# Four edits to a one-core kernel of eight layers: operand fills, a store queue, a causal mask and the spreading of routing weights

## The chip, the cores and the metric

The kernel runs on one core of a Trainium2 chip, in one launch. The metric is device time in microseconds, the median of several runs. Before the change three runs took 2757.15, 2762.11 and 2770.57 us; the median is 2762.11.

The engines are named as in the profile: PE is TensorE (matrix products and transposes), DVE is VectorE, ACT is ScalarE, POOL is GpSimd and SP is SyncE, which here only issues DMA transfers. In the code they are called PE, V, S, G and nc.sync; nc.scalar.dma_start puts a transfer on ScalarE's own queue (ACTq).

## What is computed

The input x has 32 sequences of 64 tokens with 256 channels, so 2048 rows of 256 float32 numbers; ctx has the same shape. Eight residual layers follow each other:

```python
x = x + L0_xattn(layernorm(x), ctx, ctx, gamma)
x = x + L0_ffn(layernorm(x), ...)          # silu(gate) * up, then down
x = x + L1_xattn(layernorm(x), ctx, ...)   # 16 heads, quantised q, k, v and weights
x = x + L1_ffn(layernorm(x), ...)          # causal attention with rotary embedding, then 4 experts
x = x + L2_xattn(layernorm(x), ctx, ...)   # banded attention
x = x + L2_ffn(layernorm(x), ...)          # quantised gated unit
x = x + L3_xattn(layernorm(x), ctx, ctx)   # sigmoid attention
x = x + L3_ffn(layernorm(x), ...)          # 8 routed experts and a shared one
```

Three of them are touched by the change:

```python
# L0_xattn: 8 heads of 8 over the 64 rows of a sequence; attention runs over the 256 columns
qk = einsum('bhdq,bhdl->bhql', qh, kh) / sqrt(8)
ret = gamma * einsum('bhql,bhdl->bhdq', softmax(qk), vh)

# L1_ffn, attention: 16 heads of 128 over the 64 tokens of a sequence
scores = where(causal, einsum('bhqd,bhkd->bhqk', rope(q), rope(k)) / sqrt(128), lowest)
out = einsum('bhqk,bhkd->bhqd', softmax(scores), v) @ wo + bo

# L3_ffn: top 2 of 8 experts of width 176, and a shared expert of width 352
scores = softmax(x @ gate_w.T); topk_w, topk_i = top_k(scores, 2)
eo = einsum('eni,eih->enh', silu(x @ w_gate[e]) * (x @ w_up[e]), w_down)
y = einsum('ne,enh->nh', combine, eo) + (silu(x @ sw_gate) * (x @ sw_up)) @ sw_down
```

Here combine holds, for each token, its two weights at the places of its two experts and zero elsewhere.

## The kernel before, in words

The 2048 rows lie in SBUF as 16 tiles (NT) of 128 tokens, in 4 groups (NG) of 512. The layers are stages named A to H: A is L0_xattn, B L0_ffn, C L1_xattn, D L1_ffn (attention, then experts), E L2_xattn, F L2_ffn with G (L3_xattn) interleaved, H L3_ffn. The weights of a stage are requested while the stage ahead of it runs.

**Stages A and E** share attention_slots (L339), which is a manual schedule: the order of each engine's instructions is the order in which the Python code emits them, 8 slots per tile. For tile i, prepare starts 2 slots ahead, the scores for the row maxima (score_maxima, L235, products L251, reductions negm L255) start at slot 16, the attention itself (attend_unit, L274, products L283) at slot 30 and the product with the values (product_unit, L301) at slot 32. Up to three tiles are thus in flight. Products in full float32 are avoided by splitting queries and keys into three bfloat16 pieces on GpSimd (stacked, L195). The pieces are written to DRAM (d3k and d3q, one transfer per piece, five for the keys and three for the queries, L212) and read back as rows of the operand tiles stk and stq (stack_rows, L215, three transfers of 24 rows each for the keys and three for the queries). All of these go through nc.sync, one after the other. The negated maximum of each row is added by the same product: it is transposed, copied by ScalarE (nmr, nm; L263, L264), split on GpSimd and sent by ScalarE's queue into rows 96 to 98 of stq (L271). The operand tiles have 128 rows. There are four pairs, used in turn (i % 4), and operand_buffers (L152) fills their rows 64 to 127 once, stk with 1.0 and stq with 0.0. In A, VectorE does so by V.memset (L158), within prepare of tiles 0 to 3 (L432). In E the fill is a transfer from a row tile that first_of_E makes (L1293 to L1296). DMA transfers signal their end through semaphores that they share in turn, so a transfer also waits for the previous one on its own semaphore. ScalarE's other work at A's start is small: the copies of the transposed context into vmo (L457), the maxima (L263, L264, L271), and then the exponentials L287.

**D's attention** (run_D_attention, L1028) is not in a manual schedule: the framework's scheduler orders each engine's instructions from the dependencies. It has 64 units, 16 heads by 4 groups. The loop emits for unit u: product of u-4, transposed of u-3, scores of u-2, output, projections of u, inputs of a later group, values. In scores (L1094) a mask product of the identity with a bfloat16 mask tile, causalb (L1039), opens the accumulation of sp, and the four 128x128 score products add to it (L1100). VectorE takes the maximum (L1102), subtracts it (L1104), ScalarE takes the exponential of all 512 columns in one instruction (L1105), and VectorE sums (L1107), takes the reciprocal (L1108) and multiplies (L1109). transposed (L1112) then needs s on TensorE. In projections (L1073), VectorE forms rtq and rtk (L1084), and ScalarE writes the half-swapped copies rwq and rwk (L1087, two instructions each). ScalarE also copies v (L1071), pT (L1118) and oT (L1133), and in the first units hnT (L949).

**F and H.** F's parts are issued from a table (L1669 to L1688). Towards its end it also steps the first routing of H (routed_H for group 0), and the generator owners (L1757, by way of heads["owner"] at L1683), which makes the tile owner in three ScalarE copies. owner holds, in 32-row blocks, a 1 where a column of the 1408 routed columns belongs to expert e. routed_H (L1765) normalises a group, makes xnT and the routing weights, transposes those to 8 rows of 512 tokens, and splits them in three bfloat16 pieces in the tile share (rows 0, 32 and 64 onwards). run_H (L1809) goes through 4 groups of 14 chunks of 128 columns: chunks 0 to 10 are routed experts (176 columns per expert, so that some chunks span two experts), 11 to 13 the shared one. Each chunk has the products pgate and pup (L1844), for a routed chunk the product cb of owner and share (L1848), which spreads each token's weight of the column's expert over the partitions, and the down products hout of the chunk ahead of it (L1820). ScalarE makes sl = silu(pgate) (L1852), VectorE hm = pup * sl (L1854) and for a routed chunk hm * cb (L1856). After chunk 13 VectorE adds hout to x (L1827), and at the very end of the program 16 transfers write the output (L1892).

Of the kernel before, what the change touches and what calls it, by code (L numbers as in the profile page):

```python
# [17 lines left out]
P = 128  # L18
T = 2048
D = 256  # L20
# [11 lines left out]
def tile_net(ctx: ExitStack, tc: tile.TileContext, a: dict, out: bass.AP):  # L32
# [119 lines left out]
    def operand_buffers(pool, k, b, row=None):  # L152

        pair = {}
        for kind, value in (("k", 1.0), ("q", 0.0)):
            pair[kind] = pool.tile([P, 16, D], BF, name=f"st{kind}{b}")
            if row is None:
                V.memset(pair[kind][64:P], value)  # L158
            else:

                nc.sync.dma_start(pair[kind][64:P], bc(row[kind][64:P], 1, [64, 16, D]))
            yield
# [31 lines left out]

    def stacked(pool, k, dram, src, kind, i):  # L195
# [15 lines left out]
        for t in range(n):  # L211
            nc.sync.dma_start(d3[t].rearrange("d h c -> h d c"), t3[:, t % 3, :])  # L212
        return d3

    def stack_rows(k, d3, kind, i):  # L215
        st = k["st"][i % 4][kind]
        for m in range(3):
            first = 0 if kind == "q" else m
            src = d3[first : first + 3].rearrange("t d h c -> (t d) (h c)")
            nc.sync.dma_start(st[24 * m : 24 * m + 24], src)  # L220
# [807 lines left out]
    def run_D_attention(w, side, hs):  # L1028
# [4 lines left out]
        with ExitStack() as es:  # L1033
# [5 lines left out]
            causal = tpool.tile([P, 4, P], BF, name="causalb")  # L1039
            V.tensor_copy(causal, bc(w["causal"], 1, [P, 4, P]))  # L1040
# [53 lines left out]
            def scores(u):  # L1094
                qr, kr = qks.pop(u)
                sp = psum.tile([P, 4, P], F32, tag="sp", name="sp")
                PE.matmul(sp, identb, causal, start=True, stop=False, skip_group_check=True)
                for j in range(4):
                    js = slice(j * P, (j + 1) * P)
                    PE.matmul(sp[:, j, :], qr[:, js], kr[:, js], start=False, stop=True, skip_group_check=True)  # L1100
                mx = pool.tile([P, 4], F32, name="mx")
                V.tensor_reduce(mx, sp, AX.X, ALU.max)  # L1102
                s = pool.tile([P, 4, P], F32, name="s", bufs=3)
                V.tensor_tensor(s, sp, bc(mx, 2, [P, 4, P]), ALU.subtract)  # L1104
                S.activation(s, s, AF.Exp, scale=scale)  # L1105
                sm = pool.tile([P, 4], F32, name="sm")
                V.tensor_reduce(sm, s, AX.X, ALU.add)  # L1107
# [178 lines left out]
    def first_of_E(w, psum):  # L1286
# [5 lines left out]
        for kind, value in (("k", 1.0), ("q", 0.0)):  # L1292
            row[kind] = cp.tile([P, D], BF, name=f"row{kind}")  # L1293
# [139 lines left out]
    def run_F(w, side):  # L1433
# [12 lines left out]
        with tc.tile_pool(name="Ft", bufs=1, side=side) as tpool, tc.tile_pool(  # L1446
# [231 lines left out]
            for t in range(NT + 8):  # L1678
                for part, lag in parts:
                    if 0 <= t - lag < NT and (with_g or not part.__name__.startswith("g_")):  # L1680
                        part(t - lag)
                    if with_g and t >= NT + 1 and part.__name__ == "gained":
                        next(heads.get("owner", head), None)  # L1683
# [44 lines left out]
    def load_H(wp):  # L1728
# [18 lines left out]
        owner = w["owner"] = wp.tile([96, 1408], BF, name="owner")  # L1747
        heads["owner"] = owners(owner)

        w["xnT"], w["share"] = [], []  # L1750
        for b in range(2):
            w["xnT"].append(wp.tile([P, 2, 512], F32, name=f"xnT{b}"))
            w["share"].append(wp.tile([96, 512], BF, name=f"share{b}"))
# [3 lines left out]
    def owners(owner):  # L1757
        for t in range(3):
            rows = slice(32 * t, 32 * t + 32)
            S.copy(  # L1760
                owner[rows].rearrange("p (e i) -> p e i", i=176), bc(ident[rows, 32 * t : 32 * t + 8], 2, [32, 8, 176])
            )
            yield

    def routed_H(w, g, pool, psum, tags, big):  # L1765

        xnT, sh = w["xnT"][g % 2], w["share"][g % 2]
        if g < 2:
            G.memset(sh, 0.0)
# [29 lines left out]
        src = tp[0:8].rearrange("e j t -> e (j t)")  # L1799
        r = pool.tile([8, 512], F32, name="shr")  # L1800
        t = pool.tile([8, 512], BF, name="sht")
        S.copy(sh[0:8], src)
        V.tensor_tensor(r, src, sh[0:8], ALU.subtract)
        G.tensor_copy(t, r)
        G.tensor_copy(sh[32:40], t)
        G.tensor_tensor(sh[64:72], r, t, ALU.subtract)
        yield

    def run_H(w, side):  # L1809


        with ExitStack() as es:
            pool = es.enter_context(tc.tile_pool(name="Hw", bufs=2, side=side))
            psum = es.enter_context(tc.tile_pool(name="Hp", bufs=1, space=PSUM))
            owner = w["owner"]
            for _ in heads.pop("owner"):
                pass
            def down(g, ch, m, hm, outs):
                for j in range(4):
                    PE.matmul(  # L1820
                        outs[j // 2][:, j % 2, :], hm[:m, j * P : (j + 1) * P], w["down"][:m, ch, :],
                        start=ch == 0 and j % 2 == 0, stop=ch == 13, skip_group_check=True,
                    )
                if ch == 13:
# [9 lines left out]
            for g in range(NG):  # L1834
# [133 lines left out]
```

## Time and profile before

| measure | value |
|---|---|
| median of three runs | 2762.11 us (2757.15 to 2770.57) |
| the profiled execution | 2769.85 us, of which its span is 2768.1 us |
| ACT busy in the span | 1532.9 us |
| mean granted TensorE clock | 0.977 of full |
| DMA | 227.89 MB moved, mean 82 GB/s |
| first 25 us | PE busy 0.36, DVE 13.18, ACT 0.00, POOL 14.31 us |
| 25 to 60 us | PE busy 18.65, DVE 30.95, ACT 3.29, POOL 10.73 us |
| 60 to 280 us (rest of A) | PE busy 208.61 us of 220 |
| 1204 to 1820 us (D's attention) | PE busy 602.68, DVE 338.68, ACT 331.80, POOL 340.35 us of 616 |
| 2270 to 2430 us (late F) | PE busy 117.46 us of 160, granted clock 0.89 |

The profile is of one execution, and its times count from the start of the span. The page gives for each engine its busy time, and then the span in 40 equal slices of 69 us, each digit being the busy share of one slice in tenths (9 is 90% or more). A timeline row gives start, duration, engine, line, operation, the tile written and the tiles read, the shape and how many instructions were folded into the row; in brackets stands how long the engine had been idle before, and what released it. Durations of matrix products overlap, since TensorE has the next under way before the last has left: two starts in a row tell what a product costs, its duration does not. In the rows for windows the columns are the length and the busy time of PE, PEld (weight loads), DVE, ACT and POOL with the numbers of instructions, then the granted clock, the share of the DMA engines' time and GB/s.

### The profile page before, as it was taken

The numbers are of one execution on the slowest core, as the hardware profiler recorded it, in microseconds if no ns is written. First come the engines' busy times: TensorE is split into PE (matmuls) and PEld (weight loads), VectorE is DVE, ScalarE is ACT, GpSimd is POOL, SyncE is SP. The second block draws the span as 40 slices with busy tenths as digits, with TensorE's granted clock in tenths as the row PEclk, the third lists the DMA queues.
The fourth block names the chain that finished last, engine by engine and source line by source line (L and its number), as shares of the span: only waits on it lengthen the run. The fifth ranks groups of instructions, "written<-read, shape, count | busy, mean of one in ns | idle before, by whom it ended". The sixth has DMA issues, their size and how long they took to land.

```text
span 2768.1 us, 44270 instructions
## 1 busy us (share of the span) xinstructions
PE 2414.7 (87%) x15971; PEld 1431.1 (52%) x16078; DVE 1856.7 (67%) x3913; ACT 1532.9 (55%) x2181; POOL 1534.5 (55%) x1764
## 2 busy tenths in 40 slices
PE   4999889777777777779999999999888877789999
PEld 2555344344444444436666666666555544455565
DVE  7878555799999999955454554655577758833232
ACT  1666321699999999836555555534254557731111
POOL 4565533588888888865555555513488866710000
PEclk9999999999999999989999999999999998989999
DMA  6543000599999999930000000051343311000000
GB/s 166 133 116 86 24 1 1 120 204 204 202 204 200 203 206 201 204 106 1 16 8 23 8 1 1 1 107 52 79 99 90 93 46 55 1 0 8 8 8 8
DMA packets 618919, 227.89 MB, mean 82 GB/s; under 512 B 547494, under 2 KB 608844, under 8 KB 614092
## 3 DMA queue, kind: packets, MB, share of 16 engines
q1 hardware_dynamic: 615628, 224.26, 37.1%
q8 instruction: 127, 2.08, 0.3%
q10 hardware_dynamic: 3072, 0.79, 0.2%
q14 instruction: 92, 0.75, 0.1%
HBM read 66.91 MB, written 18.87 MB: 31 GB/s over the span
## 4 chain that ended last, share of the span: by engine, by line
PE 47%; DVE 19%; issue 9%; POOL 6%; ACT 2%; DMA 1%; ACTq 0%; POOLq 0%; DVEq 0%
DVE e L844 11%; PE yp L1141 4%; PE ppq L1082 4%; PE ppk L1082 4%; PE pgate L1844 4%; PE pup L1844 4%; PE hout L1820 3%; PE vp L1070 3%; POOL e L295 2%; PE sp L1100 2%; PE op L1126 2%; PE hmp L1198 2%; PE ep L1211 2%; PE sc L816 1%; PE op L805 1%
## 5 line engine op out<-in xcount | busy, mean ns | idle before, releaser
L868 ACT ACTIVATE ei<-e,nb,sq 128x2048 int16<-128x2048 f32 x256 | 535.4, 2092 | 39.6 <-DVE nb L865 35.0
L878 POOL CAST eb<-ei 128x2048 bf16<-128x2048 int16 x256 | 482.0, 1893 | 110.7 <-ACT ei L868 92.7
L816 PE MATMUL sc<-kT,qz 128*128 128x512 bf16 x930 | 281.0, 381 | 154.6 <-DVE e L844 150.6
L255 DVE TENSOR_REDUCE negm<-s 128x2 f32<-128x512 f32 (+1 forms) x512 | 300.7, 610 | 129.1 <-PE s L251 126.3
L844 DVE TENSOR_SCALAR_CACHE_REDUCE e<-sc,mx 128x1024 f32<-128x1024 f32 x256 | 326.1, 1274 | 0.4 <-DVE nb L865 0.3
L287 ACT ACTIVATE e<-s 128x1024 f32<-128x1024 f32 (+1 forms) x256 | 233.4, 916 | 152.4 <-PE s L283 103.5
L844 DVE TENSOR_SCALAR_CACHE_REDUCE e<-sc 128x1024 f32<-128x1024 f32 x256 | 312.4, 1220 | 4.8 <-PE sc L816 4.8
L816 PEld LDWEIGHTS <-qz 128*128 128x128 bf16 x1024 | 94.6, 97 | 260.0 <-issue 202.3
L251 PE MATMUL s<-stk,stq 96*128 96x256 bf16 (+1 forms) x1024 | 192.2, 271 | 41.0 <-DMA d3k<-t3k 24.6
L1090 POOL TENSOR_TENSOR rwq<-rwq,sin 128x512 f32<-128x512 f32 x64 | 81.1, 1267 | 239.2 <-ACT rwq L1087 212.3
L283 PE MATMUL s<-stq,stk 128*128 128x256 bf16 (+1 forms) x1024 | 180.8, 262 | 11.0 <-DMA d3k<-t3k 8.4
L829 PEld LDWEIGHTS <-vz 128*64 128x64 bf16 x4096 | 122.7, 109 | 113.7 <-issue 112.7
L1854 DVE TENSOR_TENSOR hm<-pup,sl 128x512 f32<-128x512 f32 (+1 forms) x56 | 38.7, 691 | 200.2 <-PE pup L1844 197.5
L1087 ACT ACTIVATE rwq<-ppq,dbq 64x512 f32<-64x512 f32 x128 | 87.4, 683 | 153.6 <-DVE rtq L1084 150.0
L1102 DVE TENSOR_REDUCE mx<-sp 128x4 f32<-128x512 f32 x64 | 44.3, 692 | 190.8 <-PE sp L1100 190.8
L829 PE MATMUL av<-eT,vz 128*64 128x128 bf16 x4096 | 163.2, 222 | 9.3 <-DMA eT<-eb 6.8
L251 PEld LDWEIGHTS <-stq 96*128 96x128 bf16 x1024 | 94.0, 101 | 131.6 <-issue 108.7
L305 PE MATMUL o<-e,vmo 128*32 128x256 f32 (+1 forms) x2048 | 150.7, 366 | 6.2 <-POOL e L295 4.8
L295 POOL TENSOR_SCALAR_AFFINE_SELECT e<-e 128x256 f32<-128x256 f32 (+1 forms) x256 | 132.9, 546 | 30.5 <-ACT e L287 30.3
L1852 ACT ACTIVATE sl<-pgate 128x512 f32<-128x512 f32 (+1 forms) x56 | 33.4, 597 | 207.9 <-PE pgate L1844 207.8
L91 POOL TENSOR_TENSOR rstd<-ve,mhalf 128x1 f32<-128x1 f32 (+1 forms) x40 | 25.9, 646 | 185.3 <-DVE ve L89 83.7
L1070 PE MATMUL vp<-Dwv,hnT 128*128 128x512 f32 x256 | 122.2, 600 | 6.1 <-ACT hnT L949 5.5
(406 smaller groups left out, 5443.1 us busy)
## 6 DMA issues: line engine op xcount, KB each, us to landing
stk<-d3k SPq DMA_DIRECT2D x96, 192.0 KB
stq<-d3q SPq DMA_DIRECT2D x96, 192.0 KB
d3k<-t3k SPq DMA_DIRECT2D x160, 64.0 KB
d3q<-t3q SPq DMA_DIRECT2D x96, 64.0 KB
eT<-eb SPq DMA_TRANSPOSE x256
fw<-in_L_ffn_w SPq DMA_DIRECT2D x3, 1024.0 KB
x<-in_x SPq DMA_DIRECT2D x16, 128.0 KB
c<-in_ctx SPq DMA_DIRECT2D x16, 128.0 KB
```

The costliest lines, as they stand in the source:

```text
L251: PE.matmul(sc[:, hh, lo:hi], qs[0:96, 2 * hp + hh, qc * P : (qc + 1) * P], ks[0:96, 2 * hp + hh, lo:hi], start=band is None, stop=True, s ...
L255: V.tensor_reduce(negm[:, qc, 2 * hp : 2 * hp + 2], sc[:, :, lo:hi], AX.X, ALU.max, negate=True)
L287: S.activation(e[:, :, lo:hi], sc[:, :, lo:hi], AF.Exp, scale=scale)
L295: G.affine_select(e[:, :, s0:s1], e[:, :, s0:s1], [[0, 4], [step, s1 - s0]], ALU.is_ge, 0.0, base=base, channel_multiplier=chan,)
L816: PE.matmul(sc[:, k0 : k0 + 512], qz[i % 2][:, h, :], kT[:, h // 2, 1024 * part + k0 : 1024 * part + k0 + 512], start=True, stop=True,)
L829: PE.matmul(av[i][r0 : r0 + 64, h // 4, :], vz[:, kt, h // 4, h % 4, :], eT[:, kt, :], start=h == 0 and kt < 2, stop=h == H - 1 and kt >= ...
L844: V.tensor_scalar(e, scs.pop((n, part)), 1.0, mx[:, 0:1] if part else LOWEST, ALU.mult, ALU.max, accum_out=mx[:, part : part + 1],)
L868: S.activation(ei, es_.pop(n), AF.Exp, bias=nb, scale=sq[i][:, h : h + 1], accum_out=sums[i][:, h : h + 1],)
L878: G.tensor_copy(eb, eis.pop(n - 1))
L1070: PE.matmul(vp, hnT[g][:, c, j * P : (j + 1) * P], wv[:, c, :], start=c == 0, stop=c == 1)
L1082: PE.matmul(pp, wt[:, c, hh * P : (hh + 1) * P], hnT[g][:, c, :], start=c == 0, stop=c == 1)
L1844: PE.matmul(pp[:m], w[nm + "s"][:, c, cols], xnT[:, c, :], start=c == 0, stop=c == 1)
```

## The change

Four edits are made together.

1. The fills of A's four operand pairs are no longer memsets on VectorE. ScalarE multiplies a tile of ones, read with a step of zero over 4096 columns, by 1.0 or 0.0.
2. For the queries of the first tile, the stores of d3q and the three loads of rows go through ScalarE's queue in place of SyncE's. Only A is meant; E is recognised by the entry "row".
3. D's mask product and the tile causalb go. VectorE adds the float32 mask to the scores as it moves them to SBUF, takes the maximum from there and multiplies it by -scale. Four exponentials on ScalarE, of 128 columns each, take that as bias and give the sums too, so the subtraction and the sum on VectorE go.
4. In H the product cb, the tile owner, its copies and the split of share go. ScalarE copies the transposed weights in float32, a transfer writes them to DRAM, and for each routed chunk one or two transfers on SP read the row of the chunk's expert back, repeated over its partitions, into wc. They are issued three chunks ahead of use. The shared chunks 11 to 13 come first in each group.

```diff
@@ operand_buffers
-                V.memset(pair[kind][64:P], value)
+                dst = pair[kind][64:P].rearrange("p h (a c) -> p (h a) c", c=P)
+                S.mul(dst, bc(ones[64:P], 1, [64, 32, P]), value)
@@ before stacked
+    def queue_of(k, kind, i):
+        return nc.scalar if kind == "q" and i == 0 and "row" not in k else nc.sync
@@ stacked
-            nc.sync.dma_start(d3[t].rearrange("d h c -> h d c"), t3[:, t % 3, :])
+            queue_of(k, kind, i).dma_start(d3[t].rearrange("d h c -> h d c"), t3[:, t % 3, :])
@@ stack_rows
-            nc.sync.dma_start(st[24 * m : 24 * m + 24], src)
+            queue_of(k, kind, i).dma_start(st[24 * m : 24 * m + 24], src)
@@ run_D_attention
-            causal = tpool.tile([P, 4, P], BF, name="causalb")
-            V.tensor_copy(causal, bc(w["causal"], 1, [P, 4, P]))
@@ scores
-                PE.matmul(sp, identb, causal, start=True, stop=False, skip_group_check=True)
                 for j in range(4):
                     js = slice(j * P, (j + 1) * P)
-                    PE.matmul(sp[:, j, :], qr[:, js], kr[:, js], start=False, stop=True, skip_group_check=True)
+                    PE.matmul(sp[:, j, :], qr[:, js], kr[:, js], start=True, stop=True)
+                s = pool.tile([P, 4, P], F32, name="s", bufs=3)
+                V.tensor_tensor(s, sp, bc(w["causal"], 1, [P, 4, P]), ALU.add)
                 mx = pool.tile([P, 4], F32, name="mx")
-                V.tensor_reduce(mx, sp, AX.X, ALU.max)
-                s = pool.tile([P, 4, P], F32, name="s", bufs=3)
-                V.tensor_tensor(s, sp, bc(mx, 2, [P, 4, P]), ALU.subtract)
-                S.activation(s, s, AF.Exp, scale=scale)
+                V.tensor_reduce(mx, s, AX.X, ALU.max)
+                V.tensor_scalar(mx, mx, -scale, None, ALU.mult)
                 sm = pool.tile([P, 4], F32, name="sm")
-                V.tensor_reduce(sm, s, AX.X, ALU.add)
+                for j in range(4):
+                    S.activation(
+                        s[:, j, :], s[:, j, :], AF.Exp, bias=mx[:, j : j + 1], scale=scale, accum_out=sm[:, j : j + 1]
+                    )
@@ first_of_E
-            row[kind] = cp.tile([P, D], BF, name=f"row{kind}")
+            row[kind] = w["k"].setdefault("row", {})[kind] = cp.tile([P, D], BF, name=f"row{kind}")
@@ run_F
-                    if with_g and t >= NT + 1 and part.__name__ == "gained":
-                        next(heads.get("owner", head), None)
@@ load_H
-        owner = w["owner"] = wp.tile([96, 1408], BF, name="owner")
-        heads["owner"] = owners(owner)
-        w["xnT"], w["share"] = [], []
-        for b in range(2):
-            w["xnT"].append(wp.tile([P, 2, 512], F32, name=f"xnT{b}"))
-            w["share"].append(wp.tile([96, 512], BF, name=f"share{b}"))
+        w["xnT"] = [wp.tile([P, 2, 512], F32, name=f"xnT{b}") for b in range(2)]
+        w["dram"] = ctx.enter_context(tc.tile_pool(name="Hd", bufs=2, space=bass.MemoryType.DRAM))
+        w["shares"] = {}
@@ routed_H
-        src = tp[0:8].rearrange("e j t -> e (j t)")
-        r = pool.tile([8, 512], F32, name="shr")
-        t = pool.tile([8, 512], BF, name="sht")
-        S.copy(sh[0:8], src)
-        V.tensor_tensor(r, src, sh[0:8], ALU.subtract)
-        G.tensor_copy(t, r)
-        G.tensor_copy(sh[32:40], t)
-        G.tensor_tensor(sh[64:72], r, t, ALU.subtract)
+        sh = pool.tile([8, 512], F32, name="sh")
+        S.copy(sh, tp[0:8].rearrange("e j t -> e (j t)"))
+        w["shares"][g] = w["dram"].tile([8, 512], F32, name="shd")
+        nc.sync.dma_start(w["shares"][g], sh)
@@ run_H
+            ORDER = [11, 12, 13] + list(range(11))
+            wcs = {}
+            def weights_of(n):
+                g, ch = divmod(n, 14)
+                ch = ORDER[ch]
+                if ch < 11:
+                    wc = wcs[n] = pool.tile([P, 512], F32, name="wc", bufs=4)
+                    e, r0 = ch * P // 176, 0
+                    while r0 < P:
+                        r1 = min(P, 176 * (e + 1) - ch * P)
+                        nc.sync.dma_start(wc[r0:r1], w["shares"][g][e : e + 1, :].to_broadcast([r1 - r0, 512]))
+                        e, r0 = e + 1, r1
...
-                    if ch < 11:
-                        cb = psum.tile([P, 512], F32, tag="cb", name="cb")
-                        PE.matmul(cb, owner[:, cols], sh, start=True, stop=True)
...
+                if n + 3 < 14 * NG:
+                    weights_of(n + 3)
                 if late is not None:
                     down(*late)
...
-                    if ch < 11:
-                        V.tensor_tensor(hm, hm, cb, ALU.mult)
+                if n in wcs:
+                    V.tensor_tensor(hm, hm, wcs.pop(n), ALU.mult)
```

The chunk loop of run_H is one loop over n from 0 to 55 afterwards, with group n // 14 and chunk ORDER[n % 14]; down takes its weights and its first and last chunk by that order.

## The prediction, made before the changed kernel ran

> **What bounds the kernel now.** I read the page first: TensorE is busy for 87% of the span, and its slices fall below 9 mainly at both ends and in the second attention. So for each edit I ask whether TensorE is the limit where it sits. Windows by stage, then the timeline inside each, answer that.
>
> ```profile
> PE 2414.7 (87%) x15971; PEld 1431.1 (52%) x16078; DVE 1856.7 (67%) x3913; ACT 1532.9 (55%) x2181; POOL 1534.5 (55%) x1764
> ...
> PE   4999889777777777779999999999888877789999
> ```
>
> Stage windows (length, then busy time of PE, PEld, DVE, ACT, POOL): the middle of D's attention and the last stage H are pure TensorE time, while ScalarE has nearly half of its time free.
>
> ```profile
> 1300.00:1700.00 400.00, 400.00 (x1762) 266.12 (x1760) 203.67 (x344) 215.09 (x344) 215.96 (x172) 1.00 0.03 10
> ...
> 2459.00:2764.00 305.00, 305.00 (x1018) 180.52 (x1016) 86.59 (x175) 46.70 (x74) 7.06 (x9) 1.00 0.02 6
> ```
>
> One unit of D's attention, from the timeline (start, duration, engine). The mask product starts at 1513.30 and the scores behind it at 1513.51; VectorE's and ScalarE's softmax hangs off it:
>
> ```profile
> 1513.30 0.38 PE L1097 MATMUL sp<-causalb,identb 128*128 128x512 bf16 x1
> 1513.51 1.05 PE L1100 MATMUL sp<-rtk,rtq 128*128 128x128 f32 x8
> ...
> 1514.60 0.69 DVE L1102 TENSOR_REDUCE mx<-sp 128x4 f32<-128x512 f32 x1 [3.33 <-PE sp L1100]
> ...
> 1516.05 0.63 ACT L1105 ACTIVATE s<-s 128x512 f32<-128x512 f32 x1 [1.61 <-DVE s L1104]
> ```
>
> The start, same view: the first scores come at 24.64, and twice TensorE stands over 6.6 us while VectorE fills operand tiles (the second pair is at 45.29 and 49.14).
>
> ```profile
> 24.64 1.01 PE L251 MATMUL s<-stk,stq 96*128 96x256 bf16 x4 [24.64 <-DMA d3k<-t3k]
> ...
> 26.87 3.47 DVE L158 MEMSET stk<- 64x4096 bf16 x1 [0.91 <-issue]
> 30.71 1.76 DVE L158 MEMSET stq<- 64x2048 uint32 x1 [0.38 <-issue]
> ...
> 33.25 1.18 PE L251 MATMUL s<-stk,stq 96*128 96x256 bf16 x4 [6.66 <-DVE negm L255]
> ...
> 51.68 1.18 PE L251 MATMUL s<-stk,stq 96*128 96x256 bf16 x4 [6.61 <-DVE negm L255]
> ```
>
> **H: weights' rows by transfers.** Removed: 44 products cb. Their row says 381 ns, but products overlap; what counts is the chunk's period. Two windows of one chunk: 5.38 us with a cb (2535.85 to 2541.23), 5.16 without (2750.34 to 2755.50). So 44 x 0.215 = 9.5 us leave a stage that is TensorE alone. Added: per chunk one or two loads on SP (256 KB in all) of a DRAM row repeated over partitions, requested three chunks, some 15 us, ahead. SP and the DMA engines are idle there (2% busy). The loads of Dwq, Dwk and Dwv (2 KB per partition, as here; issued 1200.48 to 1204.75) lie in the window 1190 to 1220, which moved 154 GB/s; at that rate 256 KB take 1.7 us, plus about 2 us from issue to use (x: issued 0.80, used 2.91). The cover is fourfold; without it a chunk would wait about 4 us. The rows of group 0 follow a store issued about where the share's cast now ends (2447.9), and are first needed three shared chunks after 2453.5. Stores of finished outputs now stand behind these loads on SP; the third group's are last delayed some 15 us before the end, which leaves them time. The multiply by wc reads SBUF instead of PSUM; its row is 688 ns, and 691 for two other sources, so nothing. The last chunk now has that multiply: hm is ready 0.7 us later, about when TensorE finishes the preceding down product (1.72 us). I take 0.1. H: -9.4 (bounds -9.6 and -8).
>
> At the end of F, three ScalarE copies of 1.36 us vanish; the one at 2425.46 delayed a hqT that TensorE waited 0.55 for. I take -0.4 (0 to -1.5). VectorE's and GpSimd's splitting of the share (0.68 + 2.35 us) ran beside.
>
> **D: mask on VectorE.** Removed: 64 mask products, 0.213 us each from start to start: 13.6 us, all in TensorE-bound time but for the first and last few. VectorE: the subtraction becomes the mask's addition (0.69 either way), the maximum reads SBUF (0.69 as for the sum at L1107), the sum (0.69) goes, a 128x4 scaling (0.17, as L89) comes: it gets 0.5 us freer. ScalarE: one 0.63 us exponential becomes four of 128 columns, each with a pointer bias and an accumulator read. No row has that form. From below: gjunk (256 columns, accumulator, no pointer) takes 0.41 from its start to the next instruction's (2410.40 to 2410.81); 128 columns fewer and a pointer make it about 0.4, four are 1.6. From above: hnT (128 columns, two pointers) 0.457 plus a read of 0.204, with no overlap, 0.66; four are 2.6. The Trainium skill speaks against this edit: "VectorE: DVE Perf Modes", section on the TRN2 errata, says of SBUF operands that "a single large tile pays it once; many small tiles pay it per-tile". "ScalarE: Activation LUTs", What ACT_TABLE_LOAD costs, prices a pointer-bias ACTIVATE at about 280 ns + 0.833 per column: 387 ns, four 1.55, plus reads as in the row 2.3. I take 1.8, nearer to gjunk, the only row with an accumulator and a like size.
>
> Who waits? Chain per unit from the end of the scores to s: before 3.75 us (1514.60 to 1518.34); after 0.73 + 0.73 + 0.23 + 1.87 + 0.21 + 0.69 = 4.5. Transposes need it about 7.6 us after the scores: hidden. On ScalarE, behind the exponentials: rwq, which waits for rtq on VectorE, which in the built order stands behind reciprocal and multiply. So ScalarE's round is exponentials 1.8 + 1.75 for these + 1.38 + 1.38 + 0.59 + 0.69 + 0.59 and gaps, 8.3 us against TensorE's new 9.10: hidden with 0.8 to spare. In the early units, without yp, TensorE needs 7.36; there the order puts rtq ahead of the reciprocal and the round is about 6.9, plus hnT copies (3.7 us per group): some waits. Exposed: the first unit, where TensorE already waited 5.56 for s (+0.7), early units (+0.7) and the last two (+0.7). D: -13.6 + 2.1 = -11.5 (bounds -13.6 and -4).
>
> **A: fills on ScalarE, first queries on its queue.** VectorE loses eight fills of 3.47 or 1.76. ScalarE gets eight of 4096 columns; CASTs of 1408 (1.36) and 512 columns (0.575) extrapolate to 3.7. The skill's "ScalarE" page, Rules for kernel authors, assigns mul to VectorE, and by work that is right: 29.6 us against 20.9. But the row says that ScalarE's first instruction came at 41.40; what matters is its order. After its table load (1.28): pair 0 until 9.4; three d3q stores of tile 0 (0.51 each on this queue, as nm's) until 11; pair 1 until 18.4; only then tile 0's three query rows (SP had issued them at 16.61). They are 1.8 later, but the key rows no longer wait on SP behind the query stores (12.3 for 15.07). Six row transfers took 9.6 us from first issue to product; three take about 2.1 + 3.7. First scores: 18.4 + 5.8 = 24.2, plus 0.4 for company: 24.6, as before (23.5 to 26.5). Leaving SP alone would have gained little too: six rows were bound by transfer.
>
> Then both stalls go, 2 x 6.3 net: attention of tile 0 (L283, first at 57.53) could start at 44.9. ScalarE stands in its way: the vmo copies wait for the transposed context (42.70 less one stall: 35.2), and pair 3 stands behind them until 42.9, so the row maxima (nmr, 44.26 before) leave 1.4 earlier instead of 6 to 12. Their rows land 1.9 after issue (sdown, which shares a semaphore with them, went 1.9 after), so attention starts near 47.9. On SP, queued behind sdown: tile 2's query stores and rows (from 49.20; now 47.7; usable 9.6 later, 57.3). Tile 2's scores came at 63.70, behind VectorE; now its rows are late next. Gain at tile 2: about 6.5 to 7; from there A is TensorE at 95% and shifts whole. A: -7 (bounds +1, if first scores come 2 us later and pair 3 costs 4.2 apiece, and -11).
>
> **Sum.** 9.4 + 0.4 + 11.5 + 7 = 28.3. Against the profiled execution (span 2768.1, 2769.85 us in all, 7.7 above the median): 2741.5, a ratio of 0.9898. On the median 2762.11: 2734.
>
> **Rivals.**
> *The start gives nothing* (16%). ScalarE's later query rows and pair 3 eat what VectorE gives. For it: 29.6 us on one in-order queue ahead of the maxima. Against: 6 us of slack at tile 2. Then -21.3 of 2769.85, on the median about 2741.
> *D gives nothing* (11%). ScalarE's round reaches 9.3 in most units: an exponential with its read at about 0.7. For: reads do not overlap in the upper bound. Against: gjunk's 0.41. Then -16.8: 2745.
> *ScalarE becomes D's limit, slower than before* (5%). Above about 0.65 us per exponential each further 0.1 costs 4 x 0.1 x 58 units = 23 us; from 0.78 everything gained is gone, at 0.9 it is +58 - 28: median near 2791. Against: both bounds lie below.
> *The edits do not what they say* (2%): the built order shows that all 64 and 44 products are gone, so only late rows in H remain; 44 waits of 0.2 us would cancel H: 2743.
>
> **How the numbers follow.** Likeliest (66%): 2734. About 0.5%, 13.8 us, is what a measurement can tell from no change. The first two rivals singly are still faster; both together (-9.8) are not. Faster 0.84, same 0.10, slower 0.06. The range goes from all bounds at their best (35 us, and some noise) to the start and half of D failing: 2723 to 2753.
>
> **What would show it.** H: chunk period 5.16 in all 56, no wait of hm for wc. D: unit period 9.10, DVE reciprocal waiting on ACT, TensorE at 100%; an exponential with its read near 0.4. Early D: sTp's wait about 6.3. A: first scores near 24.6, no 6.6 us waits on negm, L283 near 48, then a wait for tile 2's rows. Wrong if D's unit is above 9.2, if first scores come after 27, or if sl or hm waits for DMA in H.

## The result, and the profile after

The changed kernel took 2740.53 us (four runs, 2737.80 to 2742.99) against 2763.26 us before (four runs). The ratio is 0.9916 with a 95% interval of 0.989 to 0.9943, so 23 us or 0.84% are gained. The prediction was 2734 us, a ratio of 0.9898, with 2723 to 2753 as its range. The profiled execution took 2737.80 us.

The page after, its engine line and TensorE's row of slices:

```profile
PE 2382.9 (87%) x15866; PEld 1411.4 (52%) x15970; DVE 1822.3 (67%) x3900; ACT 1621.9 (59%) x2634; POOL 1523.5 (56%) x1750
...
PE   4999889777777777779999999999898886889999
```

TensorE's busy time fell by 31.8 us and ScalarE's rose by 89; TensorE's share of the span is the same 87%. The line numbers of a row are those of its own kernel, so the same instruction has another number before, after and in each experiment. The windows of the middle of D's attention and of H (length, then busy time of PE, PEld, DVE, ACT, POOL):

```profile
1300.00:1700.00 400.00, 400.00 (x1760) 264.86 (x1760) 203.21 (x353) 265.16 (x661) 220.58 (x176) 1.00 0.03 10
2459.00:2720.00 261.00, 261.00 (x866) 156.24 (x865) 76.93 (x159) 42.86 (x67) 0.00 (x0) 1.00 0.15 46
```

Both are still TensorE time from end to end: no new wait has taken the place of the products that left. One unit of D's attention, from the timeline (start, duration, engine):

```profile
1505.64 1.06 PE L1103 MATMUL sp<-rtk,rtq 128*128 128x128 f32 x8
...
1506.73 0.69 DVE L1105 TENSOR_TENSOR s<-sp,causal 128x512 f32<-128x512 f32 x1 [3.12 <-PE sp L1103]
...
1507.46 0.69 DVE L1107 TENSOR_REDUCE mx<-s 128x4 f32<-128x512 f32 x1
...
1508.09 1.26 POOL L1095 TENSOR_TENSOR rtk<-rtk,rwk 128x512 f32<-128x512 f32 x1
1508.18 1.20 DVE L1108 TENSOR_SCALAR mx<-mx 128x4 f32<-128x4 f32 x1
...
1509.47 0.40 ACT L1111 ACTIVATE s<-s,mx 128x128 f32<-128x128 f32 x1 [2.31 <-DVE mx L1108]
...
1509.78 0.18 ACT L1111 ACTIVATION_READ_ACCUMULATOR s<-s,mx 128x1 f32 x1
1509.87 0.39 ACT L1111 ACTIVATE s<-s,mx 128x128 f32<-128x128 f32 x1
...
1514.74 1.06 PE L1103 MATMUL sp<-rtk,rtq 128*128 128x128 f32 x8
```

The scores of the next unit start 9.10 us later, where it was 9.31. An exponential with its read takes 0.40 us from start to start: the read lies beside the next exponential. The 128x4 scaling, priced at 0.17 us, takes 1.20 here, and it ends together with GpSimd's instruction, to 0.03 us.

TensorE at the start:

```profile
24.52 1.01 PE L257 MATMUL s<-stk,stq 96*128 96x256 bf16 x4 [24.52 <-DMA x<-in_x]
...
47.91 0.61 PE L289 MATMUL s<-stq,stk 128*128 128x256 bf16 x2 [3.20 <-DMA stq<-nm]
...
56.46 0.61 PE L257 MATMUL s<-stk,stq 96*128 96x256 bf16 x2 [4.34 <-DMA stq<-d3q]
```

The two stalls of over 6.6 us on negm are gone. In their place are a wait for the maxima's rows (3.20) and, at 56.46, one for tile 2's query rows (4.34).

Where the two profiled executions differ, from the starts of the same products in both timelines:

| product | before | after | difference |
|---|---|---|---|
| first scores of tile 0 | 24.64 | 24.52 | -0.1 |
| first scores of tile 2 | 61.79 | 56.46 | -5.3 |
| B's first transposes of hdn | 278.76 | 274.15 | -4.6 |
| D's first scores | 1225.28 | 1220.12 | -5.2 |
| D's last yp | 1819.19 | 1805.62 | -13.6 |
| E's first mask product | 1962.98 | 1944.57 | -18.4 |
| H's first pgate | 2453.50 | 2433.29 | -20.2 |
| H's first hout | 2463.47 | 2440.26 | -23.2 |
| H's last hout | 2763.90 | 2731.58 | -32.3 |

The profiled pair differs by 32 us and the medians by 23. Two steps of the table have no edit in them, D's end to E (4.8) and pgate to hout at H's start (3.0). There the granted clock differs: 0.94 before and 0.98 after in the stretch from 1820 to 1990, and 0.72 before and 0.94 after in 30 us around H's start. The profiles of all the kernels below, which have these steps in common, show that it is the clock: from D's last yp to E's first mask product the changed kernel took 139.0 us with none of it at half clock, and the others 140.6, 142.1 to 142.3 or 143.8 with 3.4, 6.8 or 10.2 us at half clock, whichever edits they had. From H's first pgate to its first hout every kernel that was at full clock there took 6.97 us. Over the 24 runs of the kernel before that came with the first four experiments, the time goes with the mean granted clock (0.977 to 0.983, correlation -0.78, 1.45 us per 0.001). The profiled execution before had 0.977 and the one after 0.981, which is some 6 us. So stages are compared below by their products and the whole by medians.

### The profile page after: what moved, and what is told of

It is laid out like the page before. It is cut to its first block, busy times and chain, and to the rows that moved or that the text cites. A ratio compares the mean times of both kernels' runs of the same rounds, so it can differ in the third digit from the quotient of the medians.

```text
span 2735.8 us, 44662 instructions
## 1 busy us (share of the span) xinstructions
PE 2382.9 (87%) x15866; PEld 1411.4 (52%) x15970; DVE 1822.3 (67%) x3900; ACT 1621.9 (59%) x2634; POOL 1523.5 (56%) x1750
## 4 chain that ended last, share of the span: by engine, by line
PE 45%; DVE 20%; issue 9%; POOL 5%; ACT 3%; DMA 1%; ACTq 0%; POOLq 0%; DVEq 0%
DVE e L850 12%; PE yp L1147 4%; PE ppq L1086 4%; PE ppk L1086 4%; PE hout L1820 4%; PE pgate L1844 4%; PE pup L1844 4%; PE vp L1074 3%; PE sp L1103 2%; POOL e L301 2%; PE op L1132 2%; PE ep L1217 2%; PE hmp L1204 2%; PE sc L822 1%; PE op L811 1%
## 5 line engine op out<-in xcount | busy, mean ns | idle before, releaser
L1105 DVE TENSOR_TENSOR s<-sp,causal 128x512 f32<-128x512 f32 x64 | 44.3, 692 | 166.5 <-PE sp L1103 166.5
L1111 ACT ACTIVATE s<-s,mx 128x128 f32<-128x128 f32 x256 | 99.6, 390 | 80.5 <-DVE mx L1108 80.5
```

## The experiments

### Each edit alone

The first three kernels are the one before with one group of hunks of the diff above: edit 4, edit 3, or edits 1 and 2.

H alone.

> Only edit 4 (routing weights by transfers). Theory (the edits add up, each within its own stage; the rest of what the two profiled executions differ by is granted clock): H gets 9.1 us shorter from its first down product to the end, as in the changed kernel, and the whole about 9.5 us (ratio near 0.9966). Rival (the edits help each other: with the owner copies and the splitting gone, late F and H's start are shorter too, as the profiled pair shows 3 us more between late F and H's first down product, and 5 us more between the second attention and E): this edit alone gives 14 us or more (ratio 0.995 or less).

Measured: 2753.38 against 2763.37 us, ratio 0.9966 (0.9954 to 0.9978), so 9.4 us. From the first to the last hout its stage is 9.1 us shorter (291.32 against 300.43), as it is in each of the ten kernels here with edit 4. The theory stands; 14 us (0.9949) lies outside the interval.

D alone.

> Only edit 3 (mask on VectorE). Theory: the steady unit falls from 9.31 to 9.10 us and the stage loses part of it again in its first six units, where ScalarE's hnT copies stand behind four exponentials; the attention stage gets about 8.4 us shorter (ratio near 0.997). Rival of the prediction on record: only 2 us are given back, so 11.5 us. Rival (the experts and E behind it get shorter too, 5 us more): 13 us or more, and the experts' stretch is 5 us shorter at the same granted clock.

Measured: 2754.43 us, ratio 0.9965 (0.9951 to 0.9979), so 9.7 us with 6 to 13 possible. In its profile the attention gets 7.0 us shorter, from the first scores to the last yp. The experts behind it do not get shorter (0.0 us), so the 4.8 us in the table above are not the edit's. The interval doesn't part 8.4 from 11.5; the products of the stage do.

A alone.

> Only edits 1 and 2 (fills on ScalarE, first queries on its queue). Theory: attention of tile 0 starts 9.6 us earlier, tile 2's rows are then late and the scores of tile 2 come 5.3 us earlier; the whole gains 4 to 5 us (ratio near 0.9984). Rival (prediction on record): 7 us. Rival (the wait for tile 2's rows and later waits of L289 for transfers eat all of it): 0 to 1 us.

Measured: 2759.97 us, ratio 0.9988 (0.9978 to 0.9999), so 3.3 us. Tile 0's attention starts at 47.01 and tile 2's scores at 54.94. 7 us lies outside the interval, and so, only just, does nothing at all; the second rival's 1 us lies inside. The three ratios multiply to 0.9919, against 0.9916 measured for the change: the edits add up.

The fills alone, without the move to ScalarE's queue:

```diff
-                V.memset(pair[kind][64:P], value)
+                dst = pair[kind][64:P].rearrange("p h (a c) -> p (h a) c", c=P)
+                S.mul(dst, bc(ones[64:P], 1, [64, 32, P]), value)
```

> Edit 1 alone: fills on ScalarE, tile 0's query stores and rows on SP as before. Theory (six rows were bound by their transfer and by the queue they stand in, and the three that ScalarE issues come 1.8 us later than SP could issue them): first scores within 1 us of 24.5, the rest as with both, so the same 4 to 5 us. Rival (the key rows that no longer wait on SP are what keeps the start from getting later): first scores at 26 or later and 2 us of the gain gone.

Measured: 2759.99 us, ratio 0.9986 (0.9975 to 0.9996), the same as with both; here the interval leaves out 1 us as well. TensorE's three waits of its start:

```profile
23.36 1.01 PE L253 MATMUL s<-stk,stq 96*128 96x256 bf16 x4 [23.36 <-DMA d3k<-t3k]
...
47.00 0.61 PE L285 MATMUL s<-stq,stk 128*128 128x256 bf16 x2 [3.45 <-DMA stq<-nm]
...
55.78 0.61 PE L253 MATMUL s<-stk,stq 96*128 96x256 bf16 x2 [4.33 <-DMA d3k<-t3k]
```

First scores and tile 0's attention come within 0.1 us of the kernel with both (23.42 and 47.01 in that profile). Tile 2's scores come 0.8 later than there (54.94), but in the changed kernel, which has both edits too, they come at 56.46. So the move of the queries to another queue is worth nothing that can be seen, and the gain of A is the fills'.

### What limits A's start now

SP in the changed kernel, from the timeline: sdown, the last of B's weights, and behind it tile 2's query pieces and rows.

```profile
39.11 0.55 SPq L482 DMA_DIRECT2D wdown<-in_L_ffn_down_w  x1
44.79 0.32 SPq L106 DMA_DIRECT2D sdown<-in_L_ffn_down_s  x1
45.21 1.82 SPq L218 DMA_DIRECT2D d3q<-t3q  x3
47.08 1.73 SPq L226 DMA_DIRECT2D stk<-d3k  x3
48.98 1.18 SPq L226 DMA_DIRECT2D stq<-d3q  x3
```

SP stands still from 39.7 to 44.8. The profile puts this wait down to the transfers of the maxima (stq<-nm), which have no data in common with sdown; the first of them signals its end on the same semaphore. It was so in the kernel before:

```profile
SPq L106 <- DMA stq<-nm: 5.7, 1, 5.7
```

ScalarE issues these transfers from 42.90 on, and sdown goes 1.9 us later. Two kernels take one of the two causes away each: B's weights are requested later, or pair 3 is filled earlier.

```diff
-                if i == 3:
+                if i == 6:
                     pending.pop()()
```

> The changed kernel with B's weights requested at tile 6 in place of tile 3. Theory (tile 2's query stores and rows stand on SP behind sdown, which cannot be issued before 44.8 us): without these loads ahead of them the rows of tile 2 are there by about 45 us, the wait of 4.3 us of tile 2's scores goes, tile 2 starts near 52 in place of 56.5, and the whole gains about 4 us more against the changed kernel. Rival (the wait is the transfers' own: the DMA engines are busy and the rows come 9 us after GpSimd's pieces wherever they stand): tile 2's scores within 1 us of 56.5, no gain. Rival (the loads only collide later): the gain at tile 2 is given back where they are now issued, near 85 us.

```diff
-                if i < 4:
-                    for _ in operand_buffers(cp, k, i):
+                for b in ((i,), (i,), (2, 3))[i] if i < 3 else ():
+                    for _ in operand_buffers(cp, k, b):
                         pass
```

> The changed kernel with pair 3 filled right behind pair 2 (from 28 us on, where ScalarE is idle) in place of ahead of tile 0's maxima. Theory: nmr leaves near 37.6 in place of 42.2, the 3.2 us wait of tile 0's attention goes and it starts near 43.5 in place of 47.9; but tile 2's rows stay where they are, so the scores of tile 2 come no earlier than 55.5 and the whole gains 0 to 1.5 us. sdown shares a semaphore with the maxima's transfers: if that is what holds it, it now goes near 40 and tile 2's rows come 4 us earlier, and the gain is about 4 us. Rival (attention's start is the limit): 4 us gained even with tile 2's scores late.

Measured with late weights: ratio 0.9908 (0.9891 to 0.9926), and 2742.06 us against 2743.82 us for the changed kernel on the same chip, no difference that the intervals show. Tile 2's scores start at 52.58 and their wait is gone, as the theory said. The weights are now requested on SP from 78.8 to 84.5, and TensorE, whose next product starts at 91.43, has waited 3.3 us for an exponential of ScalarE, which it does not do in the changed kernel. ScalarE was held up by its own queue: issuing the three transfers of a tile's maxima took it 5.97 us from 84.34 on, where tile 0's took 2.44 in the changed kernel. From within that wait on, TensorE was at half clock, from 89.9 to 96.7. So the second rival, that the gain is given back near there, is the likeliest; that these loads cause the wait was not tried. The first theory's 4 us of the whole did not come.

Measured with the early pair: ratio 0.9909 (0.9893 to 0.9926), 2741.78 us. Nmr leaves at 37.17, tile 0's attention starts at 44.19, and sdown goes at 42.24 in place of 44.79: sdown waits for the first of the maxima's transfers in both kernels. The last of the 16 completions on their semaphore came at 42.22 here and at 44.77 there, 0.02 us ahead of sdown. But that transfer, issued at 37.83, took 4.4 us to land in place of 1.9: the DMA engines were busy all of the time from 36 to 40, when B's weights came in, and had 2% to do from 42 to 44, when it went in the changed kernel. Tile 2's scores come at 54.23 after a wait of 5.6 us. Neither kernel alone is rid of its wait: with late weights one comes back near 90 us, with the early pair it stays at tile 2.

### The three edits together, and the changed kernel again

The third edit is in D. Scale is applied as the mask is added and the maximum is written negated, so the 128x4 scaling goes:

```diff
-                V.tensor_tensor(s, sp, bc(w["causal"], 1, [P, 4, P]), ALU.add)
+                V.scalar_tensor_tensor(s, sp, scale, bc(w["causal"], 1, [P, 4, P]), ALU.mult, ALU.add)
-                V.tensor_reduce(mx, s, AX.X, ALU.max)
-                V.tensor_scalar(mx, mx, -scale, None, ALU.mult)
+                V.tensor_reduce(mx, s, AX.X, ALU.max, negate=True)
```

The exponential loses its scale. With both edits of A's start:

> The changed kernel with both of these, and with D's softmax without the 128x4 scaling: VectorE multiplies by scale as it adds the mask (one instruction, as before), the maximum is written negated, and the exponential needs no scale. Theory: A gains 5 to 8 us by the two; in D the scaling's 0.17 to 1.28 us leave the chain from scores to exponential in every unit, the steady unit stays at 9.10 us (TensorE is the limit), and the first units gain 1 to 2 us. Together 6 to 10 us under the changed kernel, ratio to before near 0.989. Rival (A is limited by transfers as such): under 3 us.

> The changed kernel again, on the same chip as its variants. Both theories: as before, a ratio of 0.9916 within its interval; it is the base for the others of this call.

Measured: 2733.31 us, ratio 0.9884 (0.9869 to 0.9899), against 2743.82 us and 0.9916 (0.9901 to 0.9931) for the changed kernel on the same chip. The intervals do not meet: this version beats both kernels, by 10.5 us the changed one. Tile 2's scores start at 49.55 (changed kernel here: 56.57), and TensorE's waits in the first 80 us come down to these (us in total, how often, the longest):

```profile
PE s L257 <- DMA c<-in_ctx: 24.0, 1, 24.0
PE s L257 <- DVE negm L261: 3.3, 12, 0.7
PE s L289 <- DMA stq<-nm: 1.2, 1, 1.2
PE nmT L265 <- ACT vmo L463: 0.6, 2, 0.5
```

The wait near 90 us stays, with 2.6 us. In the profiles, A up to B's first transposes is 5.2 us shorter than in the changed kernel's second execution (242.9 against 248.1 us from the first scores), and D's attention 4.9 (582.0 against 586.9); these two make up what the whole gained.

The D edit alone, to part it from A's:

> The changed kernel with the scale folded into the mask's addition and the maximum written negated, so that D's 128x4 scaling goes; nothing else. Theory (the scaling, 0.17 us by itself, ends with GpSimd's instruction whenever it meets one, 0.57 us in the median and 1.28 at most, and stands in the chain to the exponentials): the steady unit stays at 9.10 us, the first eight units gain 2 to 4 us against the changed kernel, ratio to before near 0.9905. Rival (a few tenths per unit are hidden everywhere): no gain, 0.9916.

Measured: 2738.10 us, ratio 0.9901 (0.9886 to 0.9917). The whole does not part it from the changed kernel. The stage does: between the first unit's scores and the ninth's it gains 3.9 us on the changed kernel's second execution, both with 6.8 us of the stretch at half clock. Then both take 9.10 us per unit, and in the last units another 1.0 is gained.

### Two prices in D, one in H

One exponential of 512 columns, with the mask still on VectorE:

```diff
-                V.tensor_scalar(mx, mx, -scale, None, ALU.mult)
+                V.tensor_tensor(s, s, bc(mx, 2, [P, 4, P]), ALU.subtract)
+                S.activation(s, s, AF.Exp, scale=scale)
                 sm = pool.tile([P, 4], F32, name="sm")
-                for j in range(4):
-                    S.activation(...)
+                V.tensor_reduce(sm, s, AX.X, ALU.add)
```

> The changed kernel with one exponential of 512 columns in D: VectorE adds the mask, takes the maximum, subtracts it and sums after the exponential, so the scaling and the four small exponentials go and VectorE has one more 0.69 us instruction than the kernel before. Theory (taking the mask product from TensorE is what gains; the four exponentials are hidden but cost the first units): steady unit 9.10 us, VectorE about 5.3 us busy per unit, the first eight units gain 2 to 3 us against the changed kernel, ratio near 0.9908. Rival (VectorE's added work makes the chain of the first units as long again): same as the changed kernel or 1 us slower.

Measured: 2743.36 us, ratio 0.9915 (0.9898 to 0.9933). By the whole the same as the changed kernel: the rival's outcome. The unit is 9.10 us, so the gain is indeed the mask product's removal, and the split exponential neither gains nor costs there. In the profile the attention is 2.7 us shorter than in the changed kernel's second execution (584.2 against 586.9), 2.3 of them in the last five units and 0.5 in the first eight, though 3.4 us more of them were at half clock; the whole cannot show so little. The subtraction is the surprise, in VectorE's timeline of this kernel:

```profile
1500.32 0.80 DVE L1108 TENSOR_TENSOR s<-s,mx 128x512 f32<-128x512 f32 x1
...
1509.42 1.26 DVE L1108 TENSOR_TENSOR s<-s,mx 128x512 f32<-128x512 f32 x1
...
1518.52 1.73 DVE L1108 TENSOR_TENSOR s<-s,mx 128x512 f32<-128x512 f32 x1
```

It took 0.69 before, reading PSUM and SBUF; reading SBUF twice it takes 1.17 in the median (0.68 to 1.80).

ScalarE made slower, by copying each stretch of s onto itself twice behind its exponential (as built, two exponentials come first and then their four copies):

```diff
                         s[:, j, :], s[:, j, :], AF.Exp, bias=mx[:, j : j + 1], scale=scale, accum_out=sm[:, j : j + 1]
                     )
+                    for _ in range(2):
+                        S.copy(s[:, j, :], s[:, j, :])
```

> The changed kernel with two more copies of 128 columns on ScalarE behind each exponential of D (each copies a stretch of s onto itself), so that an exponential with its read costs near 0.97 us in place of 0.385. It prices the rival on record that ScalarE becomes D's limit. By the prediction's round (each 0.1 over 0.65 costs 23 us): unit near 10.4 us, 75 us slower than the changed kernel. Theory now: ScalarE stands idle 2.7 us of each steady unit, and the built order puts VectorE's rtq ahead of the reciprocal, so that ScalarE's wait for rtq goes; the unit stays between 9.10 and 9.3 us, and only the first units lose, 5 to 15 us in all.

Measured in one run: 2746.71 us. Four exponentials with their copies took 3.26 us (1510.40 to 1513.66), 0.81 each, not 0.97 as expected. That is beyond the 0.78 at which the recorded rival had everything gained gone. The steady unit is still 9.10 us:

```profile
1300.00:1700.00 400.00, 400.00 (x1760) 264.69 (x1759) 200.99 (x352) 334.46 (x1011) 220.92 (x176) 1.00 0.03 10
```

ScalarE has 69 us more to do in these 400 and TensorE does not notice. What gave way shows in ScalarE's waits over the same 400 us, first in the changed kernel, then in this one:

```profile
ACT rwq L1091 <- DVE rtq L1088: 75.7, 44, 2.0
ACT s L1111 <- DVE mx L1108: 58.2, 45, 2.3
```

```profile
ACT s L1111 <- DVE mx L1108: 59.1, 44, 2.2
```

The wait for rtq, 1.7 us per unit, is gone, because the scheduler put rtq ahead of the reciprocal on VectorE. The 5 to 15 us that the first units were expected to lose did not come either: the attention took 586.1 us, against 586.9 in the changed kernel's second execution.

A single buffer for H's rows:

```diff
-                    wc = wcs[n] = pool.tile([P, 512], F32, name="wc", bufs=4)
+                    wc = wcs[n] = pool.tile([P, 512], F32, name="wc", bufs=1)
-                if n + 3 < 14 * NG:
-                    weights_of(n + 3)
+                weights_of(n)
```

> The changed kernel with a single buffer for wc, so that the next chunk's weights are requested only when the present chunk's multiply is done. Theory (a row is there 2.7 to 2.9 us after its issue, inside the 4.4 us between two multiplies): no wait of hm for wc, chunk period 5.16 us, same time as the changed kernel. Rival (the prediction's 3.7 us and company of a second load): hm waits 0.2 us or more in the chunks with two experts and the period grows with it.

Measured in one run: 2740.69 us. VectorE waited for wc once, 0.2 us, in 44 chunks, and from the first to the last hout H took the same 291.32 us. The theory stands: the depth of three chunks is not needed, since the last packet of a chunk's 256 KB ends 2.6 to 3.2 us after the first issue (the first starts about 1.0 us after it), a little wider than the 2.7 to 2.9 expected.

## Why the prediction was right, and where it was not

The direction and the likeliest mechanism were right, and the time lies in the range, near its middle. The forecast gain of 28 us was 5 too much, from two terms.

- **H: -9.4 forecast; 9.1 in the stage, 9.4 by the median of the edit alone.** Right as summed: 44 times the difference of two chunk periods. The rows had landed before use, and the rival of late rows fell. The price of a row, 3.7 us, was too high (2.6 to 3.2): the 154 GB/s under it are the mean of a window in which the queue was idle for a good part. The fourfold cover hid that.
- **The end of F: -0.4.** Too small to be seen; the profiled pair's larger difference there goes with the granted clock.
- **D: -11.5 forecast; 8.4 in the profiled pair (7.0 with the edit alone).** The steady unit came as written (9.10), and so did the first unit's wait for s (5.6 before, 6.3 after). What failed is the term "early units (+0.7)": up to the ninth unit 2.2 us were lost where 1.7 should have been gained, so 3.9, against 1.4 forecast for the first unit and the early ones together. Four waits make 3.3 of these: 0.7 more for s in the first unit, as forecast, and then 0.96 and 1.52 us for hnT (0.21 and 0.42 before) and 0.76 for pT (none before). The rest is clock (3.4 us more at half speed there): three kernels with D as before and as much half clock took 0.3, 0.6 and 1.4 us more than the one before. The last units lost 1.2 for 0.7 forecast. The hnT copies stand on ScalarE behind rwq and the four exponentials, and these behind the scaling. Its price of 0.17 was read from L89 with GpSimd out of the way. One of L89's instructions had taken 0.72 us before the change, and it ended 27 ns after one of GpSimd's (shortest, median and longest in ns):

```profile
L89 DVE TENSOR_SCALAR ve<-mvh x4: 161/170/719, 2390.8 to 2455.0; 128x4 f32<-128x4 f32 x4
```

The removal of the scaling alone gave 3.9 us back: the waits for hnT are 0.36 and 0.32 there, and the one for pT is gone. TensorE's waits in the first units of the changed kernel:

```profile
1232.71 1.09 PE L1122 MATMUL sTp<-ident,s 128*128 128x128 f32 x4 [6.29 <-DVE s L1115]
...
1249.22 1.12 PE L1074 MATMUL vp<-Dwv,hnT 128*128 128x512 f32 x2 [0.96 <-ACT hnT L955]
...
1259.42 1.16 PE L1132 MATMUL op<-pT,v 128*128 128x128 f32 x8 [0.76 <-ACT pT L1124]
...
1284.23 1.13 PE L1074 MATMUL vp<-Dwv,hnT 128*128 128x512 f32 x2 [1.52 <-ACT hnT L955]
```

- **The exponentials.** The 1.8 us for four was near: 1.54 from start to start, 1.65 to the end of the last read. The upper bound had added the reads; they overlap.
- **ScalarE as D's limit (5%).** That rival's arithmetic kept ScalarE's 1.75 us wait for rtq as a fixed part of its round. The slowed kernel shows that it is slack: the order on VectorE changed and the wait went.
- **A: -7 forecast; 3.3 by the median of the edit alone, 4.6 in the profiled pair.** The chain to tile 0's attention was right (24.6 and 47.9 forecast, 24.52 and 47.91 measured), and so were the wait for sdown and tile 2's rows as the next limit (57.3 forecast, 56.46 measured). That 24.6 came out to 0.1 us is in part luck: of the three query rows, forecast for 18.4 with 6.2 us to the scores, ScalarE issued two at 12.68 and the third, after a wait, at 20.66, 3.9 before the scores. The step that failed is "Tile 2's scores came at 63.70": that is their second pair, and the first came at 61.79, so the same working would have given 4.5:

```profile
61.79 0.63 PE L251 MATMUL s<-stk,stq 96*128 96x256 bf16 x2
...
63.70 0.39 PE L251 MATMUL s<-stk,stq 96*128 96x256 bf16 x2
```

Of the 5.3 us that tile 2 won, 1.9 went at once: TensorE ran at half clock from 55 to 62, and so it did before until 62 (a pair took 0.63 us at 61.79 and 0.39 at 63.70). The 4.6 of the pair is one draw: from the first scores to B's first transposes the three kernels without edits 1 and 2 took 250.5 to 254.1 us, and the eight with A as in the changed kernel or with the fills alone 244.7 to 250.7, 3.6 less in the mean.

- **"Leaving SP alone would have gained little too".** Shown: with the queries left on SP the gain is the same.

What stays open: whether the edits change the granted clock. The ten kernels with edit 4 had 3 to 24 us at half clock around H's start in their profiles, 7 in the median, and the four without it 10 to 17. The medians give no sign of it, since edit 4 alone gains what its products explain. Open as well is what makes A's length differ by up to 6 us between kernels that have the same edits in it.

## What to carry to other kernels

Where a stage is one engine's time from end to end, the gain of taking work from that engine is the work's start-to-start cost times its count, and it comes out as computed; where a start-up chain is shortened, find the next late event and subtract from its own time. A wait in the middle of an in-order engine's round is not a fixed cost: ask whether the scheduler can fill it before calling that engine the limit. The shortest or median time of a small VectorE instruction on SBUF data is not its price beside GpSimd: look at the longest in its row, and at what GpSimd does at the place where the new one will stand.

## What the runs showed of the hardware

VectorE stood still for GpSimd. In the changed kernel the 128x4 scaling took 0.16 to 0.17 us in the five units in which no instruction of GpSimd was under way as it began, and from 0.17 to 1.28 us, 0.61 in the median, in the other 59; in 54 of those it ended 24 to 29 ns after GpSimd's instruction:

```profile
L1108 DVE TENSOR_SCALAR mx<-mx x64: 157/570/1276, 1229.5 to 1790.9; 128x4 f32<-128x4 f32 x64
```

In the kernel with one exponential, the subtraction of two SBUF operands ended 0.55 us after GpSimd's instruction, as if it began only then. The maximum, one SBUF operand (0.67 to 0.69 us), and the mask's addition, PSUM and SBUF (0.68 to 0.69), do not change, though GpSimd was at work beside them in all 64 units. The Trainium skill has this rule in "SBUF — State Buffer", Who interferes with whom: tensor_scalar in its two-port modes, and an instruction with two SBUF inputs against a GpSimd instruction that reads SBUF, take an exclusive lock, and the second to come blocks fully. The runs agree, in both forms; that the scaling ran in a two-port mode no trace shows.

The clock is granted in steps: in all traces it is full or half, in stretches of about 3.41 us or multiples of it. In the changed kernel it becomes half at 55.1, three microseconds into the wait of 4.34 us that ends at 56.46, and stays so until 62.0. The skill's "TensorE: Matmul & The Clock Gate", Part 1, describes such a window and says that low activity brings half rate; that stretch agrees. What brings the stretches without a wait was not looked into.

A ScalarE fill of 64x4096 took 3.60 us for either tile; VectorE's memsets had taken 3.47 and 1.76. It is slower by work, and it still won, because before the change ScalarE was idle until 41.40.
